# A graph network on one core: the second 128 rows of the first layer's weights loaded before the edge lists, and edge counting begun two products later

## The chip, the cores and the metric

The kernel runs on one core of a Trainium2 chip. A core has five engines with instruction queues of their own: TensorE (PE, with its weight loads as PEld), VectorE (DVE), ScalarE (ACT), GpSimd (POOL) and SyncE (SP), and 16 DMA engines that all queues share. The metric is the device time of one execution in microseconds (us), as the median of several runs.

## The reference

A graph of 1250 nodes with 1024 features and 41,250 directed edges (`src`, `dst`, a type 0 or 1) goes through two layers, each behind a layer norm with ReLU and added to its input.

```python
# layer 0: relational convolution; h is t5-normalised (rms) and scaled by ln_weight first
out = h @ W_root + bias
for r in range(2):
    w = (edge_type == r)
    sums = segment_sum(h[src] @ W_rel[r] * w[:, None], dst)
    out = out + sums / maximum(segment_sum(w, dst), 1.0)[:, None]
y = h + elu(out) @ wo_weight
# layer 1: graph attention
h = h @ W;  e = exp(-leaky_relu(al[src] + ar[dst], 0.1))
h_prime = segment_sum(e[:, None] * h[dst], src) / (segment_sum(e, src)[:, None] + 1e-5)
out = x + elu(h_prime)
```

F, the width of `W_root` and of each `W_rel[r]`, is 286. The three matrices are laid side by side as `w_cat`, 1024 rows of 858.

## The kernel before, in words

The nodes lie in T = 10 tiles of up to 128 rows. `fast_arm` is the path that runs; a general path behind it is entered only when the edge list does not suit the fast one. Its first stage does two things in one interleaved stream on TensorE:

- **Products** (line 728): for each tile, 16 of them (SK = 16), one for each block k of 128 rows of `w_cat` (k = 0 to 7, line 1472 loads them) and each half r of its columns. For tile 0 the order is k=0 r=0, k=0 r=1, k=1 r=0 and so on, so that a block is needed only two products after the one before it; for later tiles r is the outer loop. Each product is two instructions of 128x429 in f32. In this document products are numbered from 1: product 3 is the first that reads block k=1, product 9 the first that reads k=4.
- **Counts** (lines 527 and 530, `chunks`): the edges are 162 groups of two times 128 edges, sorted by `dst`. Each of 324 steps makes a one-hot `key` on VectorE (line 526) and multiplies it with one-hots `lo` (line 495), which adds up in PSUM how many edges of each type join each pair of nodes. The second of two groups is read out by ScalarE (line 535), two evictions for four steps. The accumulators share three PSUM banks (tag "tp") with the transposes, and one more bank takes every fourth accumulator.

How many counts follow each product is set by the formula with `late`: none before the product that `late` names, then 324 spread evenly over the products up to six before the end.

Around them lie, for each tile: statistics (line 550, VectorE), the normalised rows h (`norm`, line 565, ScalarE), four transposes at a time (`turn`, line 583), their way back into SBUF with the scale of ln_weight (`scaled`, line 590, ScalarE), and the residual (line 594): h is added to the tile's rows of x by an accumulating DMA that GpSimd issues. `first_plan` says before which product of tile 0 each of these stands, for instance statistics of tile 1 at 8 and 9, its norm at 10, its transposes at 12 and 13 and their way back at 13 and 15. `carried` (lines 646 to 654), at 6, makes what the counts need at the groups' borders; two of its parts, a cast of `firsts` (line 652) and a limit (line 650), are GpSimd's.

Order: TensorE, VectorE and ScalarE follow the program's order (`manual_schedule`). GpSimd's and SyncE's instructions are put in order by the planner that builds the program. All plain loads go through SyncE's queue, in the order of the program: the two halves of tile 0's rows (line 1470), then block k=0, then `edges` (line 484, all three lists, into `room`), then `firsts` (line 485, into `meta`), then the blocks k=1 to 7 with tile 1's rows behind k=3, the bias, and the other tiles. Before tile 0's work, twelve idle matmuls run on TensorE.

Of the kernel before, what the change touches and what calls it, by code (L numbers as in the profile page):

```python
# [19 lines left out]
def _bcast_rows(ap, n_part, width, offset=0):  # L20

    return bass.AP(tensor=ap.tensor, offset=ap.offset + offset, ap=[[0, n_part], [1, width]])
# [388 lines left out]
def fast_arm(tc, ctx, edges, firsts, w_root, conv_bias, wo, w_gat, a_gat, out,  # L411
# [7 lines left out]
    KD = D // 128  # L419
# [52 lines left out]
    with ExitStack() as c1:  # L472
# [206 lines left out]
        def clear_if_odd():  # L679

            odd = nc.values_load(n_odd, engines=[mybir.EngineType.Activation], min_val=0, max_val=8192)
            with tc.If(odd > 0):
                nc.scalar.activation(cnt_raw, eps6.to_broadcast([128, 2 * T * NPAD]), AF.Copy, scale=0.0)
# [22 lines left out]
        late_plan = {(1, 1): lambda: square(1), (1, 2): lambda: norm(2), (1, 12): lambda: square(2),  # L706
                     (2, 1): lambda: count_over(), (2, 4): lambda: turn_worst(), (2, 6): lambda: worst_over(),
                     (2, 12): lambda: clear_if_odd()}
        done, late = 0, 6
        SK = 2 * KD  # L710
        for t in range(T):
            pys[t] = ps.tile([128, 2, 512], F32, name="mm")
            for i in range(SK):

                r, k = divmod(i, KD) if t else (i % 2, i // 2)
# [16 lines left out]
                done = max(done, want)  # L732
# [689 lines left out]
@with_exitstack  # L1422
def gnn_kernel(
    ctx: ExitStack,
    tc: tile.TileContext,
    x: bass.AP,
    src: bass.AP,
    dst: bass.AP,
    etype: bass.AP,
    ln_w: bass.AP,  # L1430
    w_rel: bass.AP,
    w_root: bass.AP,
    conv_bias: bass.AP,
    wo: bass.AP,
    w_gat: bass.AP,
    a_gat: bass.AP,
    edges: bass.AP,
    firsts: bass.AP,
    w_cat: bass.AP,
    lnw_cols: bass.AP,  # L1440
    out: bass.AP,
):


    nc = tc.nc
    D = x.shape[1]
    F = w_root.shape[1]
    KD = D // 128
    assert x.shape[0] == N and 0 <= NG * GE - src.shape[0] < GE and F % 2 == 0

    const = ctx.enter_context(tc.tile_pool(name="const", bufs=1))
    big = ctx.enter_context(tc.tile_pool(name="big", bufs=1))

    def large_tiles():
        return ([big.tile([128, D + 2], F32, name=f"x{t}", tag=f"x{t}")[:, :D] for t in range(T)],
                big.tile([128, 2 * T * NPAD], F16, name="cnt", tag="cnt"),
                [big.tile([128, D + 2], F32, name=f"w{k}", tag=f"w{k}") for k in range(KD)])


    xs, cnt_raw, wt = large_tiles()  # L1460
    wcat = [w[:, :3 * F].rearrange("p (r f) -> p r f", r=2) for w in wt]

    def load_x(t):
        nc.sync.dma_start(xs[t][:ROWS[t]], x[t * 128:t * 128 + ROWS[t], :])

    def loads(part):

        if part == 0:
            for c in (slice(0, 512), slice(512, D)):
                nc.sync.dma_start(xs[0][:, c], x[:128, c])  # L1470
        for k in range(1) if part == 0 else range(1, KD):
            nc.sync.dma_start(wt[k][:, :3 * F], w_cat[k * 128:(k + 1) * 128, :])
            if k == 3:
                load_x(1)
        if part == 0:
            return
        nc.sync.dma_start(bias, _bcast_rows(conv_bias, 128, F))
        for t in range(2, T):
            load_x(t)

    eps5 = const.tile([128, 1], F32, name="eps5")
    nc.vector.memset(eps5, 1e-5)
    eps6 = const.tile([128, 1], F32, name="eps6")
    nc.vector.memset(eps6, 1e-6)
    ones = const.tile([128, 1], F32, name="ones")
    lnw = const.tile([128, KD], F32, name="lnw")
    nc.scalar.dma_start(lnw, lnw_cols)

    nc.scalar.activation(ones, eps5, AF.Sqrt)
    bias = const.tile([128, F], F32, name="bias")  # L1490
    ident = const.tile([128, 128], F32, name="ident")
    make_identity(nc, ident)
    n_odd = const.tile([1, 1], I32, name="n_odd")

    meta = const.tile([128, 2816], F32, name="meta")
    parts, at = [], 0
    for size in (NG * J, NG * J // 2, NG * T, J * 128, T * W, T, NG, NG):
        parts.append(meta[:PE_, at:at + size])
        at += size
    keys = parts[0].rearrange("p (q j) -> p q j", j=J)  # L1500
    lows = parts[1].bitcast(F16).rearrange("p (q j) -> p q j", j=J)
    hot_ck = parts[2].bitcast(BF16).rearrange("p (q c) -> p q c", c=2 * T)
    iota_lo = parts[3].bitcast(F16).rearrange("p (l j) -> p l j", j=2 * J)
    nc.vector.memset(ones, 1.0)
    iota_key, iota_ck, ck = parts[4].bitcast(F16), parts[5].bitcast(F16), parts[6]
    firsts_at = meta[:, at - NG:at].bitcast(I32)
    nc.gpsimd.iota(iota_key, pattern=[[1, 2 * T * W]], base=0, channel_multiplier=0,
                   allow_small_or_imprecise_dtypes=True)
    nc.gpsimd.iota(iota_lo, pattern=[[1, 128], [0, 2 * J]], base=0, channel_multiplier=0,
                   allow_small_or_imprecise_dtypes=True)  # L1510
    nc.gpsimd.iota(iota_ck, pattern=[[1, 2 * T]], base=1, channel_multiplier=0,
                   allow_small_or_imprecise_dtypes=True)
    nc.gpsimd.memset(cnt_raw.rearrange("p (c n) -> p c n", n=NPAD)[:, :, N:], 0.0)

    with ExitStack() as arm:
        fast_arm(tc, arm, edges, firsts, w_root, conv_bias, wo, w_gat, a_gat, out, ident, eps5, eps6, lnw, const,
                 big, wt, wcat, bias, xs, cnt_raw, meta, keys, lows, hot_ck, ck, firsts_at, n_odd, iota_lo, iota_key, iota_ck,
                 loads)

    odd = nc.values_load(n_odd, min_val=0, max_val=8192)  # L1520
    with tc.If(odd > 0):
        with ExitStack() as arm:
            xs, cnt_raw, wt = large_tiles()
            general_arm(tc, arm, x, src, dst, etype, ln_w, w_rel, w_root, conv_bias, wo, w_gat, a_gat, out,
                        ident, ones, eps5, eps6, const, [w[:, :D] for w in wt], xs, cnt_raw)
# [49 lines left out]
```

## Time and profile before

| | |
|---|---|
| Median of 3 runs | 586.63 us (586.52 to 587.97) |
| The profiled execution | 587.84 us; span of its trace 586.0 us |
| Granted TensorE clock, mean | 0.995 |
| TensorE busy | 569.8 us, 97% of the span |
| VectorE, ScalarE, GpSimd busy | 411.1, 286.7, 26.3 us |
| First product of the stage, first product of tile 2 | 8.08 us, 27.63 us |
| End of the stage (first matmul of the next, line 805) | 181.54 us |
| Mean DMA rate over the span | 75 GB/s; 273 and 343 in the first two fortieths |

A timeline line gives start and duration in us, the engine, the line of the kernel, the operation with `out<-in` by tile names, shape and count; square brackets hold the idle time before it and what ended it. `SPq` and `POOLq` are the instruction queues that issue DMAs. In a table by window the columns are the window, its length, then for PE, PEld, DVE, ACT and POOL the busy time with the number of instructions, the granted TensorE clock as a share of full speed, the mean busy share of the 16 DMA engines, and GB/s.

### The profile page before, as it was taken

What the parts mean: (1) busy time and instruction counts of PE and PEld (TensorE: products, weight loads), DVE (VectorE), ACT (ScalarE), POOL (GpSimd) and SP (SyncE); (2) the same over time, 40 slices, a digit from 0 to 9 for tenths busy, and PEclk for the clock granted to TensorE, in tenths of its full rate; (3) what the DMA queues carried; (4) which work ended last, traced back from release to release, by engine and by line L of the source; (5) the groups of instructions that cost most, each with busy time, mean ns of one, the idle gap of its engine ahead of it and who ended that gap; (6) DMA issues with size and microseconds to landing.
All of it is one profiled execution on the core that took longest, in us unless ns stands there. A gap on an engine that the chain in (4) does not pass through costs nothing. (4 is left out here: it accounts for less than half of the span.)

```text
span 586.0 us, 8877 instructions
## 1 busy us (share of the span) xinstructions
PE 569.8 (97%) x2894; PEld 412.3 (70%) x2894; DVE 411.1 (70%) x1051; ACT 286.7 (49%) x694; POOL 26.3 (4%) x41
## 2 busy tenths in 40 slices
PE   7899999999999999999999999999999999999994
PEld 5565656666656767766766788888877778888872
DVE  4789788889772766559899925141849988887732
ACT  3686776777752000003422224263636588877722
POOL 4010000000000000000000000000033000000000
PEclk9999999999999999999999999999999999999998
DMA  7951111101108500100116710000010122222211
GB/s 273 343 143 27 37 37 37 37 2 37 27 2 288 178 36 37 73 37 36 50 66 199 230 42 0 2 0 1 1 36 3 44 100 72 89 91 73 86 69 51
DMA packets 21933, 43.86 MB, mean 75 GB/s; under 512 B 2510, under 2 KB 7886, under 8 KB 21876
## 3 DMA queue, kind: packets, MB, share of 16 engines
q1 hardware_dynamic: 20308, 38.07, 18.9%
q0 software_dynamic: 1424, 5.12, 4.6%
q8 instruction: 25, 0.41, 0.3%
q14 instruction: 32, 0.26, 0.2%
q10 hardware_dynamic: 144, 0.00, 0.0%
HBM read 24.55 MB, written 13.52 MB: 65 GB/s over the span
## 5 line engine op out<-in xcount | busy, mean ns | idle before, releaser
L728 PE MATMUL mm<-w,hT 128*128 128x429 f32 (+1 forms) x320 | 145.8, 542 | 2.7 <-DMA w<-in_w_cat_dram 2.7
L535 ACT ACTIVATE cnt<-acc 128x240 f32 x162 | 63.5, 392 | 53.7 <-PE acc L527 25.2
L526 DVE TENSOR_SCALAR key<-meta 128x240 bf16<-128x240 f16 x324 | 74.3, 276 | 2.7 <-PE acc L527 1.3
L805 PE MATMUL mm<-y,cnt 128*128 128x286 bf16 (+3 forms) x600 | 75.2, 285 | 0.4 <-DVE y L621 0.4
L805 PEld LDWEIGHTS <-cnt 128*128 128x128 f16 (+1 forms) x600 | 59.5, 99 | 14.8 <-issue 1.0
L527 PEld LDWEIGHTS <-lo 128*128 128x128 bf16 x324 | 35.7, 113 | 45.3 <-issue 30.6
L527 PE MATMUL acc<-key,lo 128*128 128x240 bf16 x324 | 61.0, 268 | 1.2 <-ACT hT L590 1.1
L728 PEld LDWEIGHTS mm<-w,hT 128*128 128x128 f32 (+1 forms) x320 | 48.7, 189 | 7.2 <-issue 6.4
L495 DVE TENSOR_TENSOR lo<-meta 128x512 bf16<-128x512 f16 x81 | 34.1, 421 | 21.3 <-PE acc L530 20.3
L996 PE MATMUL mm<-w,a 128*128 128x257 f32 (+3 forms) x192 | 44.5, 379 | 0.0
L816 ACT ACTIVATE bias<-bias 128x286 f32<-128x286 f32 (+1 forms) x10 | 4.4, 442 | 80.2 <-DVE bias L815 80.2
L996 PEld LDWEIGHTS mm<-w,a 128*128 128x128 f32 (+1 forms) x192 | 35.7, 187 | 5.5 <-ACT h L1022 0.2
L851 PE MATMUL mm<-wo,meta 128*128 128x512 f32 (+1 forms) x80 | 37.6, 592 | 0.0
L1104 ACT ACTIVATE d<-meta,score 128x128 f32<-128x128 f32 x84 | 27.2, 388 | 9.9 <-DVE d L1121 9.9
L530 PEld LDWEIGHTS <-lo 128*128 128x128 bf16 x161 | 18.3, 114 | 19.0 <-issue 18.7
L1166 PE MATMUL tp<-hm,zm 128*128 128x512 f32 (+1 forms) x120 | 30.1, 400 | 0.6 <-ACT tp L1172 0.6
L530 PE MATMUL acc<-meta,lo 128*128 128x20 bf16 x161 | 29.4, 183 | 0.0
L1104 ACT ACTIVATE d<-meta,tenths 128x128 f32<-128x128 f32 x84 | 27.2, 389 | 0.0
L1166 PEld LDWEIGHTS tp<-hm,zm 128*128 128x128 f32 (+1 forms) x120 | 21.6, 184 | 6.0 <-ACT tp L1172 0.6
L1166 PE MATMUL tp<-hh,zh 128*128 128x512 f32 (+3 forms) x60 | 23.7, 395 | 0.0
L1166 PE MATMUL tp<-parts,zl 128*128 128x512 f32 (+3 forms) x60 | 23.7, 394 | 0.0
L1166 PE MATMUL tp<-hh,parts 128*128 128x512 f32 (+1 forms) x60 | 23.7, 394 | 0.0
(207 smaller groups left out, 1010.7 us busy)
## 6 DMA issues: line engine op xcount, KB each, us to landing
x<-h POOLq DMA_DIRECT2D x9, 512.0 KB, 4.5
xd<-x SPq DMA_DIRECT2D x9, 512.0 KB, 2.6
x<-in_x_dram SPq DMA_DIRECT2D x8, 512.0 KB, 11.9
w<-in_L_gnn_W_dram SPq DMA_DIRECT2D x8, 512.0 KB, 7.0
w<-in_w_cat_dram SPq DMA_DIRECT2D x8, 429.0 KB, 10.5
squares<-cnt SPq DMA_DIRECT2D x10, 320.0 KB, 3.3
d<-squares SPq DMA_DIRECT2D x40, 80.0 KB, 2.1
d<-xd SPq DMA_DIRECT2D x9, 256.0 KB, 2.7
```

The costliest lines, as they stand in the source:

```text
L495: nc.vector.tensor_tensor(los[q // 2], iota_lo, lows[:, q:q + 2, :].rearrange("p q j -> p (q j)")[:, None, :].to_broadcast([PE_, 128, 2 * J]),
L526: nc.vector.tensor_scalar(key, iota_key, keys[:, q, j:j + 1], None, op0=ALU.is_equal)
L527: nc.tensor.matmul(acc, los[q // 2][:, :, (q % 2) * J + j], key, start=(j == 0), stop=(j == J - 1))
L530: nc.tensor.matmul(*carry, start=False, stop=False)
L535: nc.scalar.activation(cnt_w[:, :, bass.ds(b, W)], a3, AF.Copy)
L728: nc.tensor.matmul(pys[t][:ROWS[t], r, :F + HF], hTs[t][0][:, k, :ROWS[t]], wcat[k][:, r, :], start=(k == 0), stop=(k == KD - 1))
L805: nc.tensor.matmul(pm[:n, r, :f], cnt[:k, h, r, t * 128:t * 128 + n], ybs[h][:k, s, r, :f], start=(h == 0 and s == 0), stop=(h == T - 1 an ...
L816: nc.scalar.activation(ex[:n], ex[:n], AF.Exp)
L851: nc.tensor.matmul(po[:n, c, :], oT[:, i, :n], wo_of[i][:, cs], start=(i == 0), stop=False)
L996: nc.tensor.matmul(o[:a.shape[2], :c1 - c0], a[:, k, :], b[k][:, c0:c1], start=(start and k == 0), stop=(k == KH - 1), skip_group_check=no ...
L1104: nc.scalar.activation(form[:, t - t0, :], rows[:, s, :], AF.Exp, bias=n[:, t:t + 1], scale=scale)
L1166: nc.tensor.matmul(sums_of[s, c][:n], at(sets[s % 2][f], t, t + 1)[:k, 0, :n], h[:k, c * HD:c * HD + HD], start=(t == 0 and f == "h"), sto ...
```

## The change

```diff
@@ -706,7 +706,7 @@
                      (2, 12): lambda: clear_if_odd()}
-        done, late = 0, 6
+        done, late = 0, 8
         SK = 2 * KD
         for t in range(T):
             pys[t] = ps.tile([128, 2, 512], F32, name="mm")
@@ -1468,7 +1468,7 @@
         if part == 0:
             for c in (slice(0, 512), slice(512, D)):
                 nc.sync.dma_start(xs[0][:, c], x[:128, c])
-        for k in range(1) if part == 0 else range(1, KD):
+        for k in range(2) if part == 0 else range(2, KD):
             nc.sync.dma_start(wt[k][:, :3 * F], w_cat[k * 128:(k + 1) * 128, :])
             if k == 3:
                 load_x(1)
```

`loads(0)` is called before the two lists are loaded, `loads(1)` behind them. With the second edit block k=1 goes ahead of `edges` and `firsts`; everything from k=2 on stays where it is. With the first, the first counts stand behind product 9 instead of product 7, and the formula's divisor falls from 148 to 146, so that the last counts stand behind the same product as before. `first_plan` is unchanged.

## The prediction

> **What bounds the kernel now.** I read the page's busy rows first, then the costliest groups, the TensorE timeline of the first 28 us, SyncE's waits with each load's time to landing, GpSimd's timeline, and a table by microsecond of the loads.
>
> ```profile
> PE 569.8 (97%) x2894; PEld 412.3 (70%) x2894; DVE 411.1 (70%) x1051; ACT 286.7 (49%) x694; POOL 26.3 (4%) x41
> ...
> L728 PE MATMUL mm<-w,hT 128*128 128x429 f32 (+1 forms) x320 | 145.8, 542 | 2.7 <-DMA w<-in_w_cat_dram 2.7
> ```
>
> TensorE (PE) is busy for 97% of the span: its queue is the bound, and the change can only move what TensorE idles. The products (two instructions each) waited 2.7 us in all for the loads of w_cat, and nothing else of size. Where:
>
> ```profile
> 8.08 1.63 PE L728 MATMUL mm<-w,hT 128*128 128x429 f32 x4
> 11.75 3.84 PE L728 MATMUL mm<-w,hT 128*128 128x429 f32 x10 [2.04 <-DMA w<-in_w_cat_dram]
> 15.43 0.47 PE L527 MATMUL acc<-key,lo 128*128 128x240 bf16 x3
> ...
> 16.80 0.97 PE L728 MATMUL mm<-w,hT 128*128 128x429 f32 x2
> ...
> 17.84 0.97 PE L728 MATMUL mm<-w,hT 128*128 128x429 f32 x2
> ...
> 19.70 0.99 PE L728 MATMUL mm<-w,hT 128*128 128x429 f32 x2 [0.68 <-DMA w<-in_w_cat_dram]
> ...
> 27.39 0.26 PE L527 MATMUL acc<-key,lo 128*128 128x240 bf16 x1 [0.83 <-ACT hT L590]
> ```
>
> Products 1 and 2 (k=0), a wait of 2.04 us for k=1, products 3 to 7, then three counts; later 0.68 us before product 11 (k=5), and 0.83 us where a count needs a PSUM bank that ScalarE has not yet emptied. Steps I use: five products in 3.68 us (11.75 to 15.43) are 0.73 each; a product with two counts is 1.04 (16.80 to 17.84), so a count is 0.155; four transposes take 0.42 (21.91 to the next product's 22.34).
>
> **When loads land.** Issue plus time to landing gives k=0 at 7.67 (1.67+6.0), edges 8.84, firsts 10.51, k=2 12.67, k=3 13.74, k=5 19.70, k=6 20.7, k=7 21.8. SyncE reuses its completion slots: each issue waits for the transfer eight before it, so the issues at 11.63, 15.04 and 16.37 date k=1, tile 1's rows and k=4. From 10 us the loads run at a full 410 GB/s, about 1.07 us for each 128 rows of weights. Two things sit between k=4 and k=5:
>
> ```profile
> 12.00:13.00 1.00, 1.00 (x4) 0.49 (x4) 0.89 (x4) 0.00 (x0) 0.38 (x2) 1.00 1.02 415
> ...
> 15.00:16.00 1.00, 1.00 (x7) 0.68 (x6) 1.00 (x4) 0.00 (x0) 0.00 (x0) 1.00 1.12 349
> 16.00:17.00 1.00, 1.00 (x6) 0.58 (x6) 1.00 (x4) 0.07 (x1) 0.00 (x0) 1.00 1.07 262
> 17.00:18.00 1.00, 1.00 (x6) 0.58 (x6) 0.92 (x5) 0.57 (x2) 0.00 (x0) 1.00 1.03 254
> 18.00:19.00 1.00, 1.00 (x5) 0.45 (x5) 0.62 (x5) 0.31 (x2) 0.00 (x0) 1.00 1.00 262
> 19.00:20.00 1.00, 0.33 (x3) 0.30 (x2) 0.99 (x5) 0.77 (x3) 0.00 (x0) 1.00 1.04 410
> ```
>
> The last column is GB/s, the one before it the share of busy DMA engines: from 15 to 19 us the engines are full but move 40% less. That is tile 0's residual, an accumulating DMA from GpSimd, which shares them with k=4 and k=5. And GpSimd sends it late, because of the lists:
>
> ```profile
> 10.57 0.64 POOL L652 CAST room<-meta 128x162 f32<-128x162 int32 x1 [7.21 <-DMA meta<-in_firsts_dram]
> 11.23 1.06 POOL L594 DMA_DIRECT2D x<-h  x1
> ```
>
> **The change, part by part.**
>
> *The load of k=1 moves ahead of edges and firsts.* It takes the place of edges and lands at about 8.8 (bounds: 8.7, one transfer behind k=0, and 10.3, if the slow microsecond at 8 us belongs to the place and not to the lists). Products 3 and 4 then follow product 2 at 9.5 and end at 11.0; at the worse bound at 11.8. Either is before k=2, for the same bytes stand ahead of k=2 as before: 12.67. So the wait of 2.04 becomes one of 1.7 us a step later. Products 5 and 6 run 12.7 to 14.15, 7 and 8 (k=3, landed 13.74) to 15.6, without counts between.
>
> *The lists come one transfer later:* edges near 10.0, firsts near 11.6. VectorE's chain from firsts to the second key took 3.7 us (10.54 to 14.26), so keys are ready from 15.3. Counting now begins behind product 9, which has k=4 to wait for (16.37 before; 16.1 to 16.4 now): TensorE asks for the first count at 16.9. But the statistics of tile 1 (first half, 0.68 us, behind its rows' landing at 15.04) now stand ahead of the first keys on VectorE: third key near 16.5. The cover is 0.4 to 1.6 us; if it goes, each late us costs one. I take nothing; bound 0.5.
>
> *Counting starts two products later.* 324 counts over 146 products instead of 148, ending at the same product: none is removed. The planner's formula gives 3, 5, 7, 9, 11 counts by products 7 to 11 before, and 3, 5, 7 by products 9 to 11 after: always four behind at first, 0.62 us of work no longer there to fill waits, paid later. Whether a product's two counts begin on an even or an odd one changes its step (0.97 or 1.04); by the formula that differs by 0.15 us over the whole stage: nothing.
>
> *On GpSimd the residual is queued behind the cast, which waits for firsts.* Cast at 11.65, issue at 12.3. When do its packets start? In the trace the rate falls just after 15.0 for an issue at 11.23: 4 us. The Trainium skill, "DMA: Bandwidth & Descriptors", section "Latency and other measured facts", puts the first byte of a GpSimd DMA at about 1 us. By the rule they would start at 13.3, ahead of k=4 and k=5 as much as before: no gain there. By the row they start at 16.3, when k=4 has just landed and most of k=5's 1.07 us can pass before. I take the row; k=5 lands at about 18.2 (bounds: 17.3 without any overlap, 19.7 as before). k=6 and k=7 have the same bytes ahead of them as before: 20.7, 21.8.
>
> *ScalarE.* It turns back tile 1's transposes (L590) behind eight evictions of counts now, of which the last began at 25.92; after the change six stand ahead of it. It starts about 25.2 instead of 26.2, and the bank it empties is asked for by a count two products later. So the 0.83 us at 27.39 should go (bounds: 0 to 0.83 gained; I take all).
>
> **The sum**, to the first product of tile 2, which starts at 27.63 now with 22 counts done. After: product 9 at 16.2, with 3 counts to 17.4; product 10 to 18.4; product 11 at 18.4 (k=5 landed), 12 to 20.5. Tile 1's normalised rows come at about 20.85 from ScalarE (two evictions at 18.4 to 19.6, then 1.22 us), so its transposes run 20.9 to 21.3 (a wait of 0.4). Product 13 with three counts to 22.5, transposes and 14 to 23.9, 15 and 16 to 26.0. Tile 2 starts at 26.0 with 18 counts done: 1.6 us earlier, less the four counts (0.6) still owed: **1.0 us gained**. Behind that TensorE is full, and its waits add to under 1 us up to 230 us, so the gain is kept to the end. The profiled execution took 587.84 with a span of 586.0, so 1.8 lies around it; it is 1.2 over the median of 586.63. The span would become 585.0, and the median 586.63 - 1.0 = **585.6**.
>
> **Rivals.**
>
> *A: the residual meets k=5 all the same* (issued on another lag, or the bank wait comes back). Product 11 then starts at 19.7 with four counts fewer done; 1.3 us of the gain goes, of which the transposes' wait hides 0.4. Time 586.5. For it: four microseconds of lag in one load are no law. Against: the second residual, issued at 21.50, has its drop after 25 us too.
>
> *B, the slower one: GpSimd's order changes.* Only TensorE, VectorE and ScalarE follow the order written by hand; GpSimd's is the planner's, which put the residual behind the cast though tile 0's rows were ready at 7.53 and firsts at 10.51. With firsts a transfer later the planner may put the residual first. It is then issued at 7.6 and its 2.6 us of every DMA engine (landing after 4.5 us where nothing else loads, less some 1.9 of start) fall on k=2, k=3, tile 1's rows and k=4: k=4 lands near 18.9. Product 9 starts at 18.9 with no count done, where it started at 16.80 with five; k=5 and the bank wait cost nothing any more. Going on as above, with 0.4 more for the late normalised rows, tile 2 starts near 28.6 with 18 counts: 1.0 late plus 0.6 owed, 1.6 us lost: 588.2. It decides from the point where k=4 lands after 17.9. For it: the rows and firsts would be only a few transfers apart; against: the cast stands first in the program.
>
> *C: the lists land later than I reckon,* at 12.6 or more, and the first counts wait for keys: 0.5 to 1 us lost off my sum, 586.4.
>
> **How the numbers follow.** My forecast 45%, A 20%, B 25%, C 10%. A measurement of this kernel can tell about 0.3% (1.8 us) from no change. My forecast's own range is 584.7 to 586.3 (k=5 at 17.3 and a shorter wait for k=2, against no bank gain). The range reaches to B with its upper bound: 584.7 to 588.6. Faster by over 0.3% (under 584.9) only if both gains are larger than reckoned: 10%. Slower by over 0.3% (over 588.4): the worse half of B and a little of C, 18%. Within: 72%.
>
> **What would show it.** Right: no wait before product 3, one of about 1.7 us before product 5, a short one before product 9, none to speak of before product 11; GB/s falling after 16 us, not 15; no wait on L590 near 26 us. Wrong: GpSimd's accumulate ahead of L652 and the rate falling before 13 us (B); product 11 still waiting to 19.7 (A); L527 waiting on keys near 17 us (C); or TensorE losing time elsewhere than in the first 30 us.

## The result, and the profile after

The changed kernel took 588.09 us as the median of 20 runs, the kernel before, in as many, 587.13 us: a ratio of 1.0015 (95% interval 1.0009 to 1.0021), 0.9 us slower. The forecast was 1.0 us faster. The whole effect lies inside the 0.3% that I had called no change, but its sign is clear and is the opposite of mine. The time lies inside my range (584.7 to 588.6) only because I had stretched that to rival B; B did not happen, so that is luck.

A word on names, which the texts above use in two ways: tile 2, tile 3 and tiles 2 to 10 count the tiles from 1, while "tile 0's" and "tile 1's" rows, squares or residual are numbered as in the code, from 0. "Tile 1's rows" are thus those of the tile whose first product is "the first product of tile 2". From here on tiles count from 1, except in the recorded expectations, which have both ways.

The two profiled executions say less than the medians. The one of after has a span of 585.6 us and took 587.41 us, 0.7 below its median; the one of before (586.0, 587.84) was 0.7 above its own. Runs of one kernel spread by about that much to each side. What follows therefore rests on where inside a trace time is won and lost, on second traces, and on ratios.

TensorE's timeline of the first 27 us, after:

```profile
8.05 6.10 PE L728 MATMUL mm<-w,hT 128*128 128x429 f32 x16
14.41 0.96 PE L728 MATMUL mm<-w,hT 128*128 128x429 f32 x2 [0.27 <-DMA w<-in_w_cat_dram]
15.21 0.47 PE L527 MATMUL acc<-key,lo 128*128 128x240 bf16 x3
...
16.58 0.97 PE L728 MATMUL mm<-w,hT 128*128 128x429 f32 x2
...
19.20 0.66 PE L583 MATMUL tp<-ident,h 128*128 128x128 f32 x4 [0.40 <-ACT h L565]
...
22.05 0.66 PE L583 MATMUL tp<-ident,h 128*128 128x128 f32 x4 [1.12 <-ACT cnt L535]
...
25.44 0.89 PE L728 MATMUL mm<-w,hT 128*128 128x429 f32 x2
```

Sixteen instructions, that is products 1 to 8, run without a gap; the waits of 2.04 and 0.68 us for loads are gone but for 0.27 us. The wait of 0.83 us on L590 is gone too, and a new one of 1.12 us stands in its place, on an eviction (L535). Tile 2 (the last line) begins at 25.44 instead of 27.63, with 18 counts done instead of 22: 2.2 us ahead, or 1.6 with the four counts owed. I had reckoned 1.0. The lead does not last to the end of the stage. The first matmul behind it, before and after:

```profile
181.54 3.71 PE L805 MATMUL mm<-y,cnt 128*128 128x287 bf16 x29
181.49 3.71 PE L805 MATMUL mm<-y,cnt 128*128 128x287 bf16 x29
```

TensorE's waits from 30 to 185 us show part of where it went. A line gives who waited for whom, the total in us, how many times, and the longest. Before:

```profile
PE acc L527 <- ACT hT L590: 0.3, 1, 0.3
```

After:

```profile
PE acc L527 <- DVE worst L676: 0.7, 1, 0.7
PE tp L583 <- ACT cnt L535: 0.6, 3, 0.2
PE acc L527 <- DVE key L526: 0.2, 1, 0.2
```

So 1.5 us are lost where 0.3 was lost before. None of these waits is for a load.

### The profile page after: what moved, and what is told of

It is laid out like the page before. It is cut to its first block, busy times and chain, and to the rows that moved or that the text cites. A ratio compares the mean times of both kernels' runs of the same rounds, so it can differ in the third digit from the quotient of the medians.

```text
span 585.6 us, 8880 instructions
## 1 busy us (share of the span) xinstructions
PE 570.4 (97%) x2894; PEld 411.9 (70%) x2894; DVE 411.1 (70%) x1051; ACT 286.8 (49%) x694; POOL 25.5 (4%) x41
## 5 line engine op out<-in xcount | busy, mean ns | idle before, releaser
L728 PE MATMUL mm<-w,hT 128*128 128x429 f32 (+1 forms) x320 | 145.2, 541 | 0.3 <-DMA w<-in_w_cat_dram 0.3
L535 ACT ACTIVATE cnt<-acc 128x240 f32 x162 | 63.4, 391 | 47.5 <-ACT cnt L535 23.9
L728 PEld LDWEIGHTS mm<-w,hT 128*128 128x128 f32 (+1 forms) x320 | 48.8, 189 | 5.5 <-issue 5.3
```

What stands on the lines that cost most here:

```text
L535: nc.scalar.activation(cnt_w[:, :, bass.ds(b, W)], a3, AF.Copy)
L728: nc.tensor.matmul(pys[t][:ROWS[t], r, :F + HF], hTs[t][0][:, k, :ROWS[t]], wcat[k][:, r, :], start=(k == 0), stop=(k == KD - 1))
```

## The experiments

**How the stage is measured.** From the step between two products in tiles 2 to 10, I take off what a step costs in the same trace when nothing waits: 0.97 us with two counts from an even one, 1.04 from an odd one, 1.10 and 1.145 with three, and 0.42 more with four transposes. What is left is called excess; it also holds waits that the listed ones miss, because a matmul's record can cover them. The table, worked out so from the TensorE timelines, gives for each trace the first product of tile 2, the counts done by then, the end of the stage and the excess.

```
kernel                    tile 2   counts   stage end   excess tiles 2-10
before                     27.63     22      181.54       1.41
before, second trace       27.27     22      181.16       1.40
order alone                26.36     22      180.28       1.42
order alone, again         26.50     22      180.42       1.42
later counting alone       26.74     18      182.40       2.74
after                      25.44     18      181.49       3.15
after, second trace        25.51     18      181.16       2.75
catch_up                   26.09     22      180.03       1.45
catch_up, again            26.62     22      180.64       1.53
worst_later                25.75     18      181.49       2.83
square_later               24.90     18      181.52       3.71
own_bank2                  27.14     18      182.76       2.71
order, late = 7            24.66     20      183.84       6.52
order, late = 9            27.56     16      185.93       5.22
```

**The two halves of the change.**

```diff
# order_only, against before
-        for k in range(1) if part == 0 else range(1, KD):
+        for k in range(2) if part == 0 else range(2, KD):
# late_only, against before
-        done, late = 0, 6
+        done, late = 0, 8
```

> The load order alone: block k=1 ahead of the lists, counting still from product 7. Theory P (phase): the loads gain in the head and what ate the gain is where the counts now fall against the transposes in tiles 2 to 9; here the counts fall as before, so the gain stays: 1.0 to 2.0 us faster than before (ratio 0.9966 to 0.9983), a step with transposes and two counts from an even one near 1.41 us as before. Rival H (head): the profiled pair is not typical and the load order itself costs; then 0.5 to 1 us slower than before (ratio 1.001 to 1.002).

> The later counting alone: loads as before, counting from product 9. P: loses 0.6 us of work that filled waits in the head, and about 1.2 us in the transposes of tiles 2 to 9: 1.0 to 1.8 us slower than before (ratio 1.0017 to 1.003). H: within 0.5 us of before (ratio 0.999 to 1.001).

Order alone: 0.9991 (0.9982 to 1.0), 586.91 us. Later counting alone: 1.002 (1.0014 to 1.0027), 588.62 us. P has both signs; the order's gain is half of what it expected. H is out in both: order alone is not slower, later counting alone is. In later counting alone the excess is 2.74 us where order alone and before have 1.4, and the new wait is the one that the trace of after shows:

```profile
50.62 0.26 PE L527 MATMUL acc<-key,lo 128*128 128x240 bf16 x1 [0.69 <-DVE worst L676]
```

By the times the order brings about 0.5 us (see the next runs for how sure that is) and the later counting costs about 1.2; together 0.7, which fits the 0.9 (0.5 to 1.2) measured for the whole.

**Both kernels once more**, unchanged.

> The kernel before once more, for a second trace of it. Both theories: ratio 1.000 within 0.0008. P: in the trace, the step from a product with two counts from an even one to the next, with four transposes between, is near 1.41 us again. H: its head is shorter than in the first trace by 0.5 us or more, with the wait of product 3 below 2.04 us, since the first trace is of an execution 0.7 us above the median.

> The changed kernel once more, for a second trace. Both: ratio near 1.0015 to before. P: the step with transposes and two counts from an even one near 1.69 us again, against 1.41 before, and tile 2 begins 1 us or more ahead of the kernel before. H: tile 2 begins no earlier than in the kernel before, since the loads land later than in the first trace.

Before: 0.9993 (0.9985 to 1.0001); after: 1.0006 (0.9998 to 1.0015). The unchanged kernel thus came out almost as far below 1 as order alone, so in this set the times alone do not tell the order's gain from nothing; the traces do show it, since order alone ends the stage at 180.28 and 180.42, before at 181.54 and 181.16. In the second traces tile 2 begins at 25.51 after and 27.27 before, as P said and H did not. The second trace of before differs from the first by a nearly constant 0.36 us from tile 2 to the end of the stage. Its wait before product 3 is shorter, as H said (of no use to H otherwise, since order alone was not slower):

```profile
11.39 3.84 PE L728 MATMUL mm<-w,hT 128*128 128x429 f32 x10 [1.62 <-DMA w<-in_w_cat_dram]
```

The step that I had expected near 1.69 us in the second trace of after has a median of 1.49: that number was one trace's. The excess is 2.75 here and 3.15 in the first trace; the difference lies in one step of tile 2. The rest of the cost repeats: against before, 0.8 us more is lost in tile 3, and 0.4 and 0.3 more in tiles 6 and 7, there in a step with transposes (in tile 6, 1.84 us instead of 1.41), while tile 4 loses 0.3 less.

**Late start, old places.** Nothing is counted before product 9, then seven counts at once, and from there the formula of before.

```diff
# catch_up, against after
-                want = min(NG * J, -(-NG * J * max(t * SK + i + 1 - late, 0) // (T * SK - 6 - late)))
+                want = min(NG * J, -(-NG * J * max(t * SK + i + 1 - 6, 0) // (T * SK - 12))) if t * SK + i >= late else 0
```

> The changed kernel, but counting follows the old formula from product 9 on: nothing before it, then seven counts at once, and from there every count behind the same product as in the kernel before. Theory P (what costs is where the counts fall against the transposes and the transposed maximum in tiles 2 to 9): the 1.3 us of those tiles go, the head keeps the order's gain: as order_only or up to 0.5 us better, ratio 0.998 to 0.9995, and every step from tile 2 on as in the kernel before. Rival W (work that filled waits in the head is missing and is paid later): the same counts are missing until product 9 and made up there at once; if that is the cost, it stays near the changed kernel, 1.0005 to 1.0015.

0.9998 (0.9989 to 1.0006), 586.89 us. The counts are as late in the head as in the changed kernel, but from tile 2 on they stand where they stood before, and the excess is back at 1.45. W's 1.0005 to 1.0015 is met by the edge of this interval alone, and not by the second measurement. Once more beside order_only:

> The load order alone once more, beside catch_up2 on one chip. Both: 0.998 to 1.000 of before. P: from tile 2 on every step as in the kernel before.

> No count before product 9, then the old formula, once more beside order_only2. P: 0.9975 to 0.9995 of before and up to 0.6 us faster than order_only2, since TensorE does not stand at product 8 for keys (0.7 us there in order_only's trace) and owes nothing afterwards. W: slower than order_only2 by 0.3 us or more.

order_only again 0.999 (0.9982 to 0.9998), catch_up again 0.9993 (0.9985 to 1.0001): not told apart, so the gain of up to 0.6 us that P gave to catch_up is not seen. The medians are 0.3 us apart the other way, which is what W had said of this pair, but that is inside the intervals. TensorE no longer stands for keys at product 8, but the step of product 9 with its seven counts and the next one take 3.3 us where 2.8 would do: the keys of that bunch are not made in time.

**Counting from product 8 and from product 10.** `late = 7` and `late = 9` in the changed kernel.

> The changed kernel with counting from product 8 (late = 7). P: the counts fall against the transposes in a third way, so the waits of tiles 2 to 9 are others than with 6 (1.4 us of excess over bare steps) and 8 (2.75 us), and need not lie between; the time is 0.9985 to 1.0015, and the trace's excess in tiles 2 to 9 accounts for the difference to order_only and to the changed kernel within 0.4 us. W: half way between order_only and the changed kernel, ratio 0.9995 to 1.0005.

> The changed kernel with counting from product 10 (late = 9). P: one more way in which counts fall against the transposes; the time can lie anywhere from 0.9985 to 1.006, and differs from the changed kernel by what the steps of tiles 2 to 9 differ. W (counts missing in the head are paid later): 0.3 us slower than the changed kernel, 1.001 to 1.002.

1.0058 (1.0044 to 1.0072), 590.48 us, and 1.0088 (1.0071 to 1.0104), 592.3 us. This decides against W: 7 does not lie between 6 and 8, and 9 is 4 us slower than 8 where W said 0.3. Counting from product 8 has the best head of all, tile 2 at 24.66, and ends the stage 2.3 us behind the kernel before. Its waits from 26 to 184 us:

```profile
PE acc L527 <- DVE key L526: 2.0, 4, 1.0
PE tp L583 <- ACT cnt L535: 1.0, 1, 1.0
PE tp L672 <- ACT cnt L535: 0.4, 1, 0.4
PE acc L527 <- ACT cnt L535: 0.4, 1, 0.4
```

and the largest of counting from product 10, two transposes that wait for a bank to be evicted, one in tile 1, one (of the maximum, L672) in tile 3:

```profile
22.42 0.66 PE L583 MATMUL tp<-ident,h 128*128 128x128 f32 x4 [2.11 <-ACT cnt L535]
...
52.56 0.27 PE L672 MATMUL tp<-ident,worst 128*1 128x128 f32 x1 [1.40 <-ACT cnt L535]
```

P's own limits, 1.0015 for the first and 1.006 for the second, were too narrow; the mechanism costs more than it said. For counting from product 8 the excess accounts for it: 6.52 less the 1.42 of order_only is 5.1; two counts more are owed, 0.3; the head is 1.7 shorter. That makes 3.7, and the stage ends 3.6 later. Counting from product 6 was not measured: counts would then stand ahead of `carried`, which makes what they need.

**Which bank.** The accumulator with a bank of its own is another one of each four.

```diff
# own_bank2, against after
-                    both = (own_bank if q % 8 == 6 else bank)("acc").rearrange("p a b -> p (a b)")
+                    both = (own_bank if q % 8 == 2 else bank)("acc").rearrange("p a b -> p (a b)")
```

> The changed kernel, but the accumulator that takes the bank of its own is the second of each four instead of the fourth: counts and transposes stay where they are, only which bank each finds changes. P: the waits of transposes on evictions (1.7 us of listed waits, 1.2 of them at the second transposes of tile 2) change by 0.5 us or more in one direction or the other. W: within 0.3 us of the changed kernel.

1.0031 (1.0019 to 1.0044), 588.63 us. No count and no transpose moved in the order. The waits of transposes on evictions went, and a longer one, of a count for a bank, appeared in tile 1:

```profile
PE acc L527 <- ACT cnt L535: 2.4, 1, 2.4
```

So which bank a count finds matters, as P said (a change of 0.5 us or more). This run shows it for the head alone: the excess of tiles 2 to 10 is 2.71, as in the changed kernel.

**Two single waits taken away.** The reading of the maximum one product later, and tile 1's squares behind two evictions instead of ahead of them:

```diff
# worst_later, against after
-                     (2, 1): lambda: count_over(), (2, 4): lambda: turn_worst(), (2, 6): lambda: worst_over(),
+                     (2, 1): lambda: count_over(), (2, 5): lambda: turn_worst(), (2, 7): lambda: worst_over(),
# square_later, against after
-            11: lambda t: square(0),
-            12: lambda t: (residual(0), turn(1, 0)),
+            12: lambda t: (square(0), residual(0), turn(1, 0)),
```

> The changed kernel with the transpose of the maximum and its reading back each one product later in tile 3 (5 and 7 instead of 4 and 6). P: the wait of 0.7 us of a count on L676 goes or shrinks and nothing else moves: 0.4 to 0.8 us faster than the changed kernel, ratio to before near 1.000. W: no change, 1.0005 to 1.0015; the time that L676 cost is lost at the next wait instead.

> The changed kernel with tile 0's squares (ScalarE, 1.05 us and two short instructions behind it, 1.55 us in all) one product later in ScalarE's order: behind the two evictions that follow the counts of product 12 instead of ahead of them. P: the wait of 1.1 to 1.2 us of the second transposes of tile 2 on an eviction falls below 0.3 us, tile 2 begins about 1 us earlier than in the changed kernel's traces, and what tiles 2 to 9 lose against bare steps stays 2.6 to 3.2 us, so the gain arrives: 0.5 to 1.0 us faster than the changed kernel, ratio to before 0.9995 to 1.0005. W: the wait moves to the next place in the head or in tile 3 and the time stays at 1.0005 to 1.0015.

1.0012 (1.0006 to 1.0019) and 1.0019 (1.0009 to 1.0029): neither is faster than the changed kernel, and P is wrong in both. Each named wait did go; the time was lost further on. In worst_later it went in the same tile, where a step with transposes took 2.17 us instead of 1.58, part of it a wait for keys:

```profile
52.59 0.45 PE L527 MATMUL acc<-key,lo 128*128 128x240 bf16 x2 [0.29 <-DVE key L526]
```

In square_later the wait of 1.12 us vanished and tile 2 began at 24.90, 0.54 ahead of after. By the second transposes among tile 2's products the lead was gone:

```profile
36.70 0.66 PE L583 MATMUL tp<-ident,h 128*128 128x128 f32 x4 [0.45 <-ACT cnt L535]
```

They begin at 36.70, the very time at which they begin in after. Half of the lead had gone before: the counts at 33.40 (33.66 in after) start 0.33 us behind the start of their keys in both traces, and VectorE, which makes the keys, has no listed idle time from 28 to 35 us in either. The rest goes in the wait shown, which is for ScalarE. Its timeline there is, in square_later (a line shorter, so that L727 is L728 elsewhere),

```profile
28.19 1.05 ACT L571 ACTIVATE sq<-h 128x1024 f32<-128x1024 f32 x1
...
29.57 1.23 ACT L565 ACTIVATE h<-x,nmr,rstd 128x1024 f32<-128x1024 f32 x1
30.70 0.77 ACT L535 ACTIVATE cnt<-acc 128x240 f32 x2
31.35 0.73 ACT L608 ACTIVATE y<-mm,rms 128x572 bf16<-128x572 f32 x1
31.97 0.93 ACT L535 ACTIVATE cnt<-acc 128x240 f32 x2
33.57 0.37 ACT L535 ACTIVATE cnt<-acc 128x240 f32 x1 [0.68 <-PE mm L727]
34.85 0.37 ACT L535 ACTIVATE cnt<-acc 128x240 f32 x1 [0.91 <-ACT cnt L535]
...
36.27 0.37 ACT L535 ACTIVATE cnt<-acc 128x240 f32 x1 [0.22 <-ACT cnt L535]
```

and in after the last eviction shown ends at the same time:

```profile
36.27 0.37 ACT L535 ACTIVATE cnt<-acc 128x240 f32 x1 [0.21 <-ACT cnt L535]
```

ScalarE works through evictions, squares, rows and parts of y without a gap from 26.0 to 32.9 us in both traces, and starts on that stretch at the same time (25.96, and 26.01 in after). After that it does stand idle, for 0.68 and 0.91 us, so it is not one full queue that holds TensorE up: TensorE, VectorE and ScalarE wait for one another in turn. W had the outcome right, though not for its reason (counts owed): a wait removed came back further on.

## Why the prediction was wrong

**The step that failed** is the sentence behind the sum: "Behind that TensorE is full, and its waits add to under 1 us up to 230 us, so the gain is kept to the end." The head did gain, more than I said. But the edit of `late` also moves the counts against the transposes in every later tile, by four counts at first and none at the end. Before, the waits of tiles 2 to 10 came to 1.4 us because counts and transposes happened to lie well; after, they come to 2.75 to 3.15. That is the last of my own signs of being wrong: TensorE losing time elsewhere than in the first 30 us. I had counted the even and odd steps of this move (0.15 us, which was right) and called the rest of it nothing. catch_up shows the cause with the later start kept: with the counts back in their old places the excess is 1.45 (1.53 in its second trace), and the time is not told from that of order alone.

**Where the loads land.** Block k=1 without a wait before product 3: right. "The same bytes stand ahead of k=2 as before: 12.67": wrong; it landed at 10.9 (issued 3.56, 7.3 to land), and the wait of 1.7 us before product 5 never came. The last number of these lines is the GB/s that the DMA engines moved from 5 to 10 us, with the lists ahead of block k=1, before:

```profile
5.00:10.00 5.00, 4.66 (x22) 3.32 (x21) 1.37 (x6) 3.99 (x11) 0.00 (x0) 1.00 0.69 238
```

and behind it, after:

```profile
5.00:10.00 5.00, 4.92 (x24) 3.64 (x24) 1.34 (x6) 3.98 (x11) 0.13 (x1) 1.00 0.84 296
```

The other traces bear this out. With the lists first the rate is 226 to 245 and k=2 lands at 12.1 to 12.7 (three traces); with k=1 first the rate is 281 to 327, but for 245 in order_only's, and k=2 lands at 10.8 to 11.4 in all eleven. So the slow stretch belonged in part to the place of the lists, and equal bytes ahead did not give an equal landing. Edges came at 9.1 and firsts at 9.8, where I had 10.0 and 11.6: C is out, and firsts were even earlier than before (10.51). Why the lists slow the queue when they come first was not tried.

**GpSimd.** Its order did not change, so B is out:

```profile
9.87 0.32 POOL L652 CAST room<-meta 128x162 f32<-128x162 int32 x1 [6.51 <-DMA meta<-in_firsts_dram]
10.53 1.06 POOL L594 DMA_DIRECT2D x<-h  x1 [0.33 <-issue]
```

The lag of about 4 us held again, where the rule of the Trainium skill that I had set beside it ("DMA: Bandwidth & Descriptors", section "Latency and other measured facts") gives about 1: the rate (last number) falls at 15 us.

```profile
14.00:15.00 1.00, 0.73 (x3) 0.41 (x3) 1.00 (x5) 0.00 (x0) 0.24 (x1) 1.00 1.10 392
15.00:16.00 1.00, 1.00 (x8) 0.62 (x6) 0.96 (x4) 0.29 (x1) 0.00 (x0) 1.00 1.08 271
```

That fall I had put behind 16 us. The issue was earlier than I reckoned (10.53, not 12.3), but the loads were earlier still: k=5 landed at 15.92, where I had 18.2, and product 11 did not wait for it. A is out as to the load; a wait for a bank did come back, at another place.

**ScalarE.** "I take all" of the 0.83 us on L590: that wait went, but the same shift put two evictions behind tile 2's rows and tile 1's squares, and tile 2's second transposes then waited 1.12 us for one of them. I looked at the wait that would go and not at what the same engine would be late with next. In square_later removing that one too gained nothing. And where the counts begin at product 7 with the new order of loads, the wait on L590 grows to 1.0 and 1.3 us (order alone, two traces): TensorE comes earlier to it, which is part of why the order brings less than the 2 us that the loads save.

**What stays open.** The second traces of before and after end the stage at the same 181.16, while the medians of 20 put after 0.9 us behind. The traces account for the lead that was lost, not for these 0.9 us. Both traces of after are of executions 0.7 us below the median of their runs; why a typical run is slower than they are was not settled.

Order alone is the only version here whose interval lies below the kernel before in one of its two measurements: 586.46 us, 0.999 (0.9982 to 0.9998).

## What to carry to other kernels

When an edit shifts one interleaved stream against another, cost it over the whole stretch in which they share banks and queues, not where it starts: here 2 us won in the first 25 us were lost again over the next 150, and one product more in the start moved the time by up to 0.7%. Where counting begins was not a knob with one direction: from product 7, 8, 9 and 10 on the ratios were 0.999, 1.0058, 1.0015 and 1.0088. So such a start is to be measured at each value; its neighbours say little. Before claiming a wait as gain, look at what the engines that feed the next steps do meanwhile; if they come no earlier, the wait only moves.

## What the runs showed of the hardware

The accumulating DMA that GpSimd issues sends its first packet 4.1 us after the issue begins while loads fill the 16 DMA engines (11.23 to 15.34 before, 10.53 to 14.67 after), and 1.4 to 1.5 us after it where the engines carry almost nothing (41.85 to 43.29 before; seven such issues). With it on the full engines the rate falls from about 410 to 260 GB/s.

From tile 2 to the end of the stage, two traces of one kernel can repeat very closely: 153.91 and 153.89 us for before, 153.92 both times for order alone. They need not: the two of after took 156.05 and 155.65, and the difference is in one step of tile 2, with the second transposes among its products, 1.81 against 1.41 us. So a difference of 0.1 us can be trusted only where a second trace has it too.
